# A transformer and expert layer in which attention scores are formed from two exact parts per operand

## The chip, the core and the metric

The kernel runs on one core of a Trainium2 chip. A core has a matrix engine (TensorE, PE in the profile, with its weight loads shown apart as PEld), VectorE (DVE), ScalarE (ACT), GpSimd (POOL) and SyncE (SP), which here only issues DMAs. Each works through its own queue in order; they meet through semaphores. TensorE writes to PSUM, 8 banks of 128 partitions by 512 float32 values. The metric is the device time of one execution in microseconds (us), as the median of several runs.

## The reference, cut to what matters

32 sequences of 256 tokens, 128 features, go through a transformer block (causal self attention, cross attention to one encoder sequence, an MLP) and then through a layer of 8 experts. The change touches the scores and softmax of the two attentions, 16 heads of 8 features:

```python
def _attn_core(q, k, v, extra_bias=None, causal_bool=False, tril_diag2_additive=False):
    w = jnp.einsum('bhqd,bhkd->bhqk', q, k) / jnp.sqrt(jnp.asarray(HD, q.dtype))
    ql, kl = (q.shape[-2], k.shape[-2])
    neg = jnp.finfo(w.dtype).min
    if causal_bool:
        mask = jnp.tril(jnp.ones((ql, kl), bool))
        w = jnp.where(mask[None, None], w, neg)
    if tril_diag2_additive:
        cm = jnp.tril(jnp.ones((ql, kl), w.dtype), k=2)
        w = w + jnp.where(cm == 0, neg, jnp.zeros((), w.dtype))[None, None]
    if extra_bias is not None:
        w = w + extra_bias[:, None, None, :]
    w = jax.nn.softmax(w, axis=-1)
    return jnp.einsum('bhqk,bhkd->bhqd', w, v)
...
a = _attn_core(split_heads(q), split_heads(k), split_heads(v), causal_bool=True)
...
a = _attn_core(split_heads(q), split_heads(k), split_heads(v), extra_bias=scorer_logits, tril_diag2_additive=True)
```

The cross attention's keys and values come from the one encoder sequence, so they are the same for all 32 sequences.

## The kernel before

**Stages.** First the attention of all 32 sequences ("batches" below), self and cross, some 880 us; then the MLP and the gate (`Chunk`), then the experts (`Experts`). The last two are not touched.

**Scores in row groups.** The 16 heads stand in 4 row groups of 4 heads (`NG`, `NJ`). A row group is 32 partitions, and one head takes all 32: 8 features times 4 rows. A float32 query or key is split into three bf16 parts (`projected`, L284 to L287, on GpSimd). Three of the four rows of a feature hold the three parts of the query; the keys repeat one part in those rows. So a head's scores take three bf16 matmuls with 32 rows, one per part of the key (`range(3)` in `maxima` and `weights`), and all nine products of parts are in. The fourth row of each feature is a spare: there masks between blocks of 64 tokens, the logits and the row maxima ride along. Within a block of 64 the causal edge is a separate bf16 matmul with the tables in `strips` (`mask_q`, `mask_k`, `by_q`, `by_k`).

Matmuls of the four row groups run in the array side by side; `issue` (L608) hands them out in turn by their column counts.

**Two passes over the scores.** `maxima` forms scores with queries on the partitions (tile `sc`), and VectorE takes the row maxima (`m`, L483). GpSimd splits them into three bf16 parts (`split`, L489 to L495), TensorE turns them (`turned_maxima`, L501), ScalarE copies them to `mT` (L502) and issues one DMA that puts them in the spare rows of `qs` (L505). `weights` forms scores with keys on the partitions, less the maxima (tile `st`), and ScalarE takes the exponential into `wt` (L545). `weighted` (L564, float32) multiplies by the values and a column of ones; `back`, `turned_back` and `joined` divide, turn and project.

**The way of queries and keys.** `projected` (L279, float32) gives 128 rows; SP stores their parts to DRAM (L290, L292), and after the store has landed loads them back spread over 32 rows per head (`load_queries` L297, `load_keys` L301). Buffers: four each of `qs` per kind of attention, `kr`, and value tiles.

**The order** is written out by hand. A half-step holds one half of an attention's `maxima` (two row groups, all or two of their heads) and one half of another's `weights`, `LAG` = 15 half-steps behind. Two half-steps are issued together (L715 to L729), all four row groups at once, then what follows them (`after`), then the side jobs that `on` and `full` have put at that step. A pair of half-steps fills up to four banks of `sc` and four of `st`, the whole of PSUM; each is free again when VectorE or ScalarE has read it. A self attention has 6 halves, a cross attention 8; in the steady part they alternate, so 14 halves or 7 pairs make a batch. Projections stand at least 8 half-steps ahead of the first use of their queries and keys.

```python
todo = [(nk, t3[:, c, :], self.qs[st, j, qb * P : qb * P + P], self.kr[st, j, part, 0:nk],
         (c, part) == (0, 0)) for c, j in enumerate(js) for part in range(3)]
for a in range(2):
    k0 = qb * P + 64 * a + 2 * self.cross
    w = min(64, nk - k0)
    todo.append((n * w, t3[:, :, k0 : k0 + w], mask_q[st, a, :],
                 by_k[st, 2 : 2 + w].unsqueeze(1).to_broadcast([32, n, w]), False))
```

Of the kernel before, what the change touches and what calls it, by code (L numbers as in the profile page):

```python
# [8 lines left out]
F32 = mybir.dt.float32  # L9
BF16 = mybir.dt.bfloat16  # L10
AF = mybir.ActivationFunctionType
ALU = mybir.AluOpType
# [7 lines left out]
HD = 8  # L20
# [8 lines left out]
V_BUFS = 4  # L29
QK_BUFS = 4  # L30
# [14 lines left out]
def transformer_moe_kernel(ctx: ExitStack, tc: tile.TileContext, ins, out: bass.AP):  # L45
# [54 lines left out]
    strips = const.tile([P, 6 * P + 2 * 66], BF16, name="strips")  # L100
    blocks = strips[:, 0 : 6 * P].rearrange("p (a n) -> p a n", n=P)
    mask_q = blocks[:, 0:2, :]
    mask_k = {False: blocks[:, 2:4, :], True: blocks[:, 4:6, :]}
    by_q, by_k = strips[:, 6 * P : 6 * P + 66], strips[:, 6 * P + 66 : 6 * P + 132]
# [5 lines left out]
    SHIFT = 4  # L110
    q_spare = {cross: const.tile([HD, S], BF16, name=f"q_spare{int(cross)}") for cross in (False, True)}
    k_spare = {}
    div32 = const.tile([P, 4], F32, name="div32")

    def query_spares(cross):
        q = q_spare[cross]
        nc.gpsimd.memset(q, 0.0)
        nc.gpsimd.affine_select(out=q, in_=q, compare_op=ALU.is_ge, fill=NEG, base=0,
                                pattern=[[1, S]], channel_multiplier=-64)
        nc.gpsimd.affine_select(out=q, in_=q, compare_op=ALU.is_ge, fill=0.0, base=SHIFT - 1,  # L120
                                pattern=[[0, S]], channel_multiplier=-1)
        if cross:
            nc.gpsimd.memset(q[0:1], 1.0)

    def key_spares(cross):
        k = k_spare[cross] = scratch([HD, 3, S], BF16, f"k_spare{int(cross)}")
        nc.gpsimd.memset(k, 0.0)
        first = k[:, 0, :]
        nc.gpsimd.memset(first, 1.0)
        for m in (1, -1):  # L130
            nc.gpsimd.affine_select(out=first, in_=first, compare_op=ALU.is_ge, fill=0.0,
                                    base=-2 * cross if m == 1 else 63 + 2 * cross,
                                    pattern=[[m, S]], channel_multiplier=-64 * m)
        nc.gpsimd.affine_select(out=first, in_=first, compare_op=ALU.is_ge, fill=1.0, base=SHIFT - 1,
                                pattern=[[0, S]], channel_multiplier=-1)

    def diagonals():
        def where(t, base, c, m, fill):

            nc.gpsimd.affine_select(out=t[0:32], in_=t[0:32], compare_op=ALU.is_ge, fill=fill, base=base - 2 * m,  # L140
                                    pattern=[[m, 66]], channel_multiplier=c)

        nc.gpsimd.memset(by_q[0:32], HIGH)
        where(by_q, 0, 2, -1, LOW)
        where(by_q, 1, 2, -1, 0.0)
        nc.gpsimd.memset(by_k[0:32], -HIGH)
        where(by_k, -2, -2, 1, -LOW)
        where(by_k, -1, -2, 1, 0.0)

        far = 200 * 31  # L150
        where(by_q, far - 2, -200, -1, LOW)
        where(by_q, far + 62, -200, -1, 0.0)
        where(by_k, far - 2, -200, -1, -LOW)
        where(by_k, far + 62, -200, -1, -HIGH)

    def diagonal_blocks():
        for a in range(2):
            nc.vector.tensor_copy(mask_q[0:32, a, 64 * a : 64 * a + 64], by_q[0:32, 2:66])
            nc.vector.tensor_copy(mask_k[False][0:32, a, 64 * a : 64 * a + 64], by_k[0:32, 2:66])
        nc.vector.tensor_copy(mask_k[True][0:32, 0, 0:66], by_k[0:32])  # L160
        nc.vector.tensor_copy(mask_k[True][0:32, 1, 66:P], by_k[0:32, 2:64])
        for g in range(1, NG):
            nc.sync.dma_start(out=strips[32 * g : 32 * g + 32], in_=strips[0:32])

    def logit_parts():

        left = scratch([1, S], F32, "left")
        parts = k_spare["logits"] = scratch([1, 3, S], BF16, "parts")
        nc.vector.tensor_scalar(left, rows[0:1, R_SC : R_SC + S], -3e38, None, ALU.max)
        for i in range(3):  # L170
            nc.vector.tensor_copy(parts[:, i, :], left)
            if i < 2:
                nc.vector.tensor_tensor(left, left, parts[:, i, :], ALU.subtract)

# [55 lines left out]
    with ExitStack() as actx:  # L230
# [24 lines left out]
        def query_rows(name):  # L255
            return dram.tile([NJ, 32, 4, S], BF16, name=name)

        def key_rows(name):
            return dram.tile([NJ, 32, 4, 3, S], BF16, name=name)

        q_rows = {cross: [query_rows(f"q{int(cross)}{i}") for i in range(QK_BUFS)] for cross in (False, True)}
        k_rows = [key_rows(f"k{i}") for i in range(QK_BUFS)]
        kx_rows = key_rows("kx")

        def fill_spare(d, src):
            n = len(src.shape) - 1
            if n == 1:
                to = d.rearrange("c (g d) i t -> d (c g) i t", d=HD)[:, :, 3, :]
# [27 lines left out]
        def load_queries(t, d):  # L296
            nc.sync.dma_start(out=t, in_=d.rearrange("c m i t -> (m i) c t"))  # L297
# [806 lines left out]
```

## Time and profile before

| | |
|---|---|
| median of 3 runs | 1452.39 us (1451.78 to 1452.43) |
| span of the profiled execution | 1451.7 us |
| granted TensorE clock, mean | 0.987 |
| TensorE busy, share of the span | 1346.3 us, 93% |
| VectorE | 1059.6 us, 73% |
| ScalarE | 870.9 us, 60% |
| GpSimd | 655.3 us, 45% |
| L483, maxima from `sc`, 896 instructions | 493.2 us busy, 607 ns each |
| L545, exponentials from `st`, 896 instructions | 419.8 us busy, 541 ns each |
| DMA | 100.22 MB, mean 69 GB/s |

The profile is of one execution. A row of instructions names its line, engine, operation, the tile written, an arrow and the tiles read, then shapes and counts; `x` counts instructions. Matmul lengths include the way through the array, so rows of one group overlap and sums of lengths exceed the time; where a rate is wanted, the distance between starts tells it. The chain of waits is followed back from the last instruction of a stretch, at each step to what released it.

### The profile page before, as it was taken

How to read it: one execution, taken by the hardware profiler on the slowest of the kernel's cores; microseconds unless marked ns; L12 is line 12 of the kernel's file. 1: busy time of each engine (PE TensorE's matmuls, PEld its weight loads, DVE VectorE, ACT ScalarE, POOL GpSimd, SP SyncE). 2: the span in 40 equal slices, each digit the busy share in tenths (PEclk: the TensorE clock that was granted, in tenths of full speed). 3: DMA queues.
4: the chain of work that ended last, by engine and by line, in shares of the span. 5: the costliest groups of instructions: out<-in, count | busy, mean ns of one | idle time of the engine just before them, and what ended most of it. 6: DMA issues, size and time to landing. Idle time of an engine off the chain costs nothing.

```text
span 1451.7 us, 55993 instructions
## 1 busy us (share of the span) xinstructions
PE 1346.3 (93%) x24028; PEld 963.8 (66%) x24028; DVE 1059.6 (73%) x2959; ACT 870.9 (60%) x2035; POOL 655.3 (45%) x1508
## 2 busy tenths in 40 slices
PE   4798989999999999999999998999899999999996
PEld 3566766776776777677677765777566666666664
DVE  6758878887878888788787761677568666666665
ACT  1366767776777777777676767877345343434343
POOL 7656455555454555545554423886311212121212
PEclk9899999999999999999999999999899999999998
DMA  6643323333242232333322115100000000000000
GB/s 179 183 125 110 112 78 116 101 105 103 86 127 90 84 123 87 109 104 101 100 79 85 35 32 142 36 2 1 1 8 8 15 8 15 8 12 11 9 15 15
DMA packets 115178, 100.22 MB, mean 69 GB/s; under 512 B 5788, under 2 KB 114672, under 8 KB 114928
## 3 DMA queue, kind: packets, MB, share of 16 engines
q1 hardware_dynamic: 104288, 91.17, 20.5%
q10 hardware_dynamic: 10640, 5.47, 1.3%
q8 instruction: 188, 3.08, 0.9%
q14 instruction: 62, 0.51, 0.1%
HBM read 54.47 MB, written 37.77 MB: 64 GB/s over the span
## 4 chain that ended last, share of the span: by engine, by line
PE 63%; DVE 24%; ACT 7%; POOL 4%; issue 2%; ACTq 1%; DMA 0%; POOLq 0%; DVEq 0%; SPq 0%
DVE m L483 14%; PE po L878 9%; PE pa L867 9%; PE pb L868 9%; PE av L564 9%; PE sc L619 8%; PE st L619 5%; ACT wt L545 4%; PE po L991 4%; PE pf L984 3%; PE pq L279 2%; DVE a L587 2%; DVE st L212 1%; DVE xn L225 1%; DVE rec L586 1%
## 5 line engine op out<-in xcount | busy, mean ns | idle before, releaser
L483 DVE TENSOR_REDUCE m<-sc 128x2 f32<-128x512 f32 (+2 forms) x896 | 493.2, 607 | 151.9 <-PE sc L619 92.0
L545 ACT ACTIVATE wt<-st 128x512 f32<-128x512 f32 (+1 forms) x896 | 419.8, 541 | 104.7 <-PE st L619 96.9
L619 PEld LDWEIGHTS <-qs 32*128 32x128 bf16 x6144 | 228.1, 94 | 108.9 <-issue 87.9
L619 PE MATMUL sc<-krx,qs 32*128 32x256 bf16 (+1 forms) x3072 | 185.7, 244 | 26.8 <-ACT xT L250 8.4
L878 PEld LDWEIGHTS po<-w,h 128*128 128x128 f32 x1152 | 155.3, 192 | 69.1 <-issue 50.1
L870 ACT ACTIVATE sa<-pa,cols 128x512 f32<-128x512 f32 x144 | 99.8, 693 | 149.2 <-PE pa L867 121.4
L872 DVE SCALAR_TENSOR_TENSOR h<-pb,cols,sa 128x512 f32<-128x512 f32 x144 | 107.9, 750 | 109.2 <-ACT sa L870 72.8
L619 PE MATMUL st<-qs,krx 32*128 32x256 bf16 (+1 forms) x3072 | 165.0, 243 | 5.9 <-DVE a L587 3.1
L619 PE MATMUL sc<-kr,qs 32*128 32x128 bf16 (+1 forms) x3072 | 164.1, 247 | 2.9 <-DMA kr<-k 1.6
L619 PE MATMUL st<-qs,kr 32*128 32x128 bf16 (+1 forms) x3072 | 160.0, 242 | 6.4 <-DVE m L483 4.3
L878 PE MATMUL po<-w,h 128*128 128x128 f32 x1152 | 162.5, 278 | 0.0
L867 PE MATMUL pa<-h_all,w 128*128 128x512 f32 x288 | 150.6, 605 | 0.0
L868 PE MATMUL pb<-h_all,w 128*128 128x512 f32 x288 | 148.5, 598 | 0.0
L892 POOL TENSOR_TENSOR z<-z 128x512 f32<-128x512 f32 x32 | 41.2, 1287 | 231.3 <-ACT z L888 231.3
L221 POOL TENSOR_TENSOR r<-r,nhalf 128x2 f32<-128x2 f32 (+1 forms) x160 | 133.7, 836 | 13.1
L619 PE MATMUL sc<-strips 32*128 32x128 bf16 (+2 forms) x1792 | 134.8, 223 | 0.1
L619 PEld LDWEIGHTS <-strips 32*128 32x128 bf16 x3584 | 127.8, 94 | 3.4 <-issue 0.5
L619 PE MATMUL st<-strips 32*128 32x128 bf16 (+2 forms) x1792 | 129.8, 222 | 0.0
L220 POOL TENSOR_SCALAR r<-mv 128x2 f32<-128x2 f32 (+1 forms) x160 | 31.1, 195 | 213.0 <-DVE mv L213 191.2
L619 PEld LDWEIGHTS <-kr 32*128 32x128 bf16 x3072 | 112.8, 93 | 14.2 <-issue 13.3
L619 PEld LDWEIGHTS <-krx 32*128 32x128 bf16 x3072 | 106.2, 93 | 13.1 <-issue 12.1
L868 PEld LDWEIGHTS pb<-h_all,w 128*128 128x128 f32 x288 | 55.2, 192 | 69.5 <-issue 58.5
(166 smaller groups left out, 2498.6 us busy)
## 6 DMA issues: line engine op xcount, KB each, us to landing
kr<-k SPq DMA_DIRECT2D x32, 768.0 KB
k<-qkp SPq DMA_DIRECT2D x32, 576.0 KB
qs<-q SPq DMA_DIRECT2D x64, 256.0 KB
q<-qkp SPq DMA_DIRECT2D x64, 192.0 KB
x<-in_x_dram SPq DMA_DIRECT2D x32, 128.0 KB
qs<-mT ACTq DMA_DIRECT2D x64, 64.0 KB
x_all<-in_x_dram SPq DMA_DIRECT2D x8, 512.0 KB
out_dram<-y SPq DMA_DIRECT2D x16, 256.0 KB
```

The source lines that it names most:

```text
L221: nc.gpsimd.tensor_tensor(r, r, nhalf[:, 0:n], ALU.pow)
L483: nc.vector.tensor_reduce(m[:, g, js[0] : js[0] + n], t3, AX.X, ALU.max, negate=True)
L545: nc.scalar.activation(w[:, 0 : n * nq], t, AF.Exp)
L564: nc.tensor.matmul(av[32 * g : 32 * g + 32, at : at + n], lhsT=self.vp[:, kb, g, WINDOW[j] : WINDOW[j] + 32], rhs=self.wts[kb, g, j], star ...
L619: nc.tensor.matmul(dst, lhsT=lhsT, rhs=rhs, start=start, stop=False, skip_group_check=True)
L867: nc.tensor.matmul(pa, lhsT=w1[:, e, 0:D], rhs=rhs, start=True, stop=True)
L868: nc.tensor.matmul(pb, lhsT=w1[:, e, D : 2 * D], rhs=rhs, start=True, stop=True)
L870: nc.scalar.activation(sa, pa, AF.Silu, bias=col(C_B1 + 2 * e))
L872: nc.vector.scalar_tensor_tensor(h, pb, col(C_B1 + 2 * e + 1), sa, ALU.add, ALU.mult)
L878: nc.tensor.matmul(po[:, i, :], lhsT=h[:, i * P : (i + 1) * P], rhs=w2[:, e, :], start=True, stop=e < NE)
L984: nc.tensor.matmul(pf, lhsT=wfc[:, f * P : (f + 1) * P], rhs=self.xT, start=True, stop=True)
L991: nc.tensor.matmul(po[:, i, :], lhsT=self.g[:, f, i * P : (i + 1) * P], rhs=wmlp[:, f, :], start=f == 0, stop=f == FF // P - 1)
```

## The change

Queries and keys become float32 tiles that hold two parts: the value rounded by a cast to float32r on GpSimd, and the float32 remainder. The four rows of a feature in a head's 32 rows hold the four pairs of parts: the query rows repeat (first, second) twice, the key rows hold (first, first, second, second). One float32r matmul per head then has all four products, where three bf16 matmuls stood. There is no spare row any more. Maxima, logits and masks are taken in by a second kind of matmul on bf16 tables of 28 rows per row group: three rows of maxima, three of logits and 22 of a staircase that forms the causal edge for a block of 44 tokens; three such blocks cover 128. They add into the same PSUM banks. `qm` holds the queries' side of the table with the maxima in its first three rows; four small DMAs per attention, issued by ScalarE, put them there. `wc` and `vc` are the tables with logits for the cross attention. Query buffers are shared by both kinds of attention (6), keys have 4, values 3, and the buffer is chosen by which is free first. `values` moves from two steps after the projections to two steps after the first half. The stores of the spare rows (`fill_spare`, `spares`, `encoder_rows`) and `max_frames` are gone.

```diff
-V_BUFS = 4
-QK_BUFS = 4
+V_BUFS = 3
+Q_BUFS = 6
+K_BUFS = 4
+M_BUFS = 2
...
+    RM, RL, R0, RS = 0, 3, 6, 22
+    NR, CW = R0 + RS, 2 * RS
+    NBLK = -(-P // CW)
...
+    def key_edges(cross, kb):
+        off = 2 * cross
+        at = kb * P
+        edges = [at - off if kb else 0] + [at + CW * b - 1 - off for b in range(1, NBLK)] + ([P - off] if kb == 0 else [])
+        return list(zip(edges, edges[1:] + [S], range(NBLK + 1)))
+
+    def query_edges(cross, qb):
+        off, nk = 2 * cross, S if qb else P + 2 * cross
+        at = qb * P + off
+        edges = [0 if cross else at] + [at + CW * b for b in range(1, NBLK)]
+        return list(zip(edges, edges[1:] + [nk], range(NBLK)))
...
-            p = wk.tile([P, n, 3, S], BF16, tag="qkp", name="qkp", bufs=2)
-            nc.gpsimd.tensor_copy(p[:, :, 0, :], x)
-            nc.gpsimd.tensor_tensor(x, x, p[:, :, 0, :], ALU.subtract)
-            nc.gpsimd.tensor_copy(p[:, :, 1, :], x)
-            nc.gpsimd.tensor_tensor(p[:, :, 2, :], x, p[:, :, 1, :], ALU.subtract)
+            p = wk.tile([P, n, S], F32R, tag="qkp", name="qkp", bufs=2)
+            nc.gpsimd.tensor_copy(p, x)
+            nc.gpsimd.tensor_tensor(x, x, p.bitcast(F32), ALU.subtract)
             for i, (_, _, _, _, d) in enumerate(todo):
...
+                to = d.rearrange("c m a t -> a (c m) t")
+                nc.sync.dma_start(out=to[0], in_=p[:, i].bitcast(F32))
+                nc.sync.dma_start(out=to[1], in_=x[:, i])
 
         def load_queries(t, d):
-            nc.sync.dma_start(out=t, in_=d.rearrange("c m i t -> (m i) c t"))
+            for b in range(2):
+                nc.sync.dma_start(out=t.rearrange("(x b) c t -> b x c t", b=2)[b], in_=d.rearrange("c m a t -> (m a) c t"))
 
         def load_keys(t, d):
-            nc.sync.dma_start(out=t.rearrange("p c j t -> p c (j t)"), in_=d.rearrange("c m i j t -> (m i) c (j t)"))
+            for a in range(2):
+                for b in range(2):
+                    nc.sync.dma_start(out=t.rearrange("(m x) c t -> x m c t", x=4)[2 * a + b],
+                                      in_=d.rearrange("c m b t -> b m c t")[b])
...
+        def max_rows(cross):
+            off = 2 * cross
+            for t in qms[cross]:
+                for kb in range(2):
+                    for lo, hi, b in key_edges(cross, kb):
+                        if b < NBLK:
+                            x = U0 + lo - kb * P + off - CW * b
+                            nc.vector.tensor_copy(t[:, :, lo:hi], u_wide[:, x : x + hi - lo].unsqueeze(1).to_broadcast([P, NJ, hi - lo]))
...
-                    todo = [(nk, t3[:, c, :], self.qs[st, j, qb * P : qb * P + P], self.kr[st, j, part, 0:nk],
-                             (c, part) == (0, 0)) for c, j in enumerate(js) for part in range(3)]
-                    for a in range(2):
...
+                    todo = [(nk, t3[:, c, :], self.qs[st, j, qb * P : qb * P + P].bitcast(F32R),
+                             self.kr[st, j, 0:nk].bitcast(F32R), c == 0) for c, j in enumerate(js)]
+                    st = slice(32 * g, 32 * g + NR)
+                    for lo, hi, b in query_edges(self.cross, qb):
+                        w = hi - lo
+                        at = qb * (P + 2)
+                        v = vc[st, at + lo : at + hi] if self.cross else v_wide[st, V0 : V0 + w]
+                        todo.append((n * w, t3[:, :, lo:hi], u_of(b)[st], v.unsqueeze(1).to_broadcast([NR, n, w]), False))
...
                 if qb:
-                    spare = self.qs.rearrange("(x i) j q -> i x j q", i=4)[3]
-                    nc.scalar.dma_start(out=spare, in_=self.mT)
+                    i = self.b % M_BUFS
+                    take(("qm", self.cross, i), self)
+                    self.qm = qms[self.cross][i]
+                    for g in range(NG):
+                        nc.scalar.dma_start(out=self.qm[32 * g : 32 * g + 3], in_=self.mT[12 * g : 12 * g + 12])
...
-                        for part in range(3):
-                            todo.append((nq, t3[:, c, :], self.kr[st, j, part, kb * P : kb * P + P],
-                                         self.qs[st, j, q0:S], (c, part) == (0, 0)))
...
+                        todo.append((nq, t3[:, c, :], self.kr[st, j, kb * P : kb * P + P].bitcast(F32R),
+                                     self.qs[st, j, q0:S].bitcast(F32R), c == 0))
+                    st = slice(32 * g, 32 * g + NR)
+                    for lo, hi, b in key_edges(self.cross, kb):
+                        w = (wc[:, kb, b, :] if self.cross else v_of(b))[st]
+                        todo.append((n * (hi - lo), t3[:, :, lo - q0 : hi - q0], w, self.qm[st, js[0] : js[0] + n, lo:hi], False))
...
-                full(e + 2, 0.55, x.values)
+                full(s + 2, 0.55, x.values)
```

Beside what the cut shows: `stairs` builds the staircase tables on GpSimd at the first step and spreads them by three DMAs; `logit_rows` fills `wc` and `vc` with some 15 copies on VectorE and 15 DMAs from SP at step 5, and `max_rows` fills the `qm` tiles with 12 copies on VectorE for each kind of attention, at steps -1 and 3.

## The prediction

> **What bounds the kernel now.** I read the stretch by engine first, then one period of the attention step by step, then the chain of waits, and last the rows that price what the change puts in. The windows view of the steady attention (120 to 840 us; columns: length, then busy time of TensorE, its weight loads, VectorE, ScalarE and GpSimd, granted clock, DMA share, GB/s):
>
> ```profile
> 120.00:840.00 720.00, 676.19 (x18400) 505.87 (x18400) 586.68 (x1473) 511.22 (x1249) 373.38 (x995) 1.00 0.31 96
> ```
>
> TensorE is busy 94%, VectorE 81%, ScalarE 71%, at full clock. A busy TensorE includes latencies, so I counted its work: in one batch (one self and one cross attention) each of the four row groups streams 22,576 columns of scores and masks. The timeline starts four 256-column bf16 matmuls, one per row group, every 0.107 us, so 0.418 ns per column, 9.4 us a batch. Seven pair steps make a batch; the same view, cut at the first score matmul of each step:
>
> ```profile
> 491.24:493.56 2.32, 2.32 (x88) 1.94 (x85) 1.45 (x4) 1.71 (x5) 0.00 (x0) 1.00 0.23 81
> 493.56:497.55 3.99, 3.89 (x111) 2.72 (x111) 3.92 (x12) 2.90 (x6) 2.05 (x8) 1.00 0.36 101
> 497.55:501.51 3.96, 3.63 (x102) 2.96 (x100) 3.50 (x6) 2.60 (x6) 1.53 (x6) 1.00 0.08 22
> 501.51:505.79 4.28, 3.83 (x99) 2.52 (x99) 3.44 (x11) 3.28 (x7) 2.99 (x4) 1.00 0.01 4
> 505.79:508.54 2.75, 2.75 (x80) 2.46 (x77) 2.02 (x6) 2.12 (x5) 2.22 (x7) 1.00 0.48 175
> 508.54:513.50 4.96, 4.04 (x99) 2.59 (x100) 2.63 (x8) 3.07 (x10) 3.43 (x11) 1.00 0.86 253
> 513.50:517.22 3.72, 3.72 (x104) 2.77 (x101) 2.75 (x6) 2.44 (x5) 1.48 (x3) 1.00 0.31 108
> sum 25.98, PE 24.19 PEld 17.96 DVE 19.73 ACT 18.10 POOL 13.70; mean PE 3.46 PEld 2.57 DVE 2.82 ACT 2.59 POOL 1.96
> ```
>
> The reader is to see that no engine bounds all steps. The second is VectorE's (3.92 of 3.99 us); the first, fifth and seventh are TensorE's. The chain of waits over the same 720 us says how much of the scores lies on the path, and the waits say who waits for them:
>
> ```profile
> by line: DVE m L483 25.0%; PE sc L619 15.2%; PE av L564 14.6%; PE st L619 9.4%; ACT wt L545 6.9%; DVE a L587 3.0%; PE pq L279 2.8%; DVE xn L225 2.0%; issue 2.0%; DVE rec L586 1.8%; DVE st L212 1.8%; ACT xT L250 1.7%; DVE h_all L225 1.7%; PE
> ```
> ```profile
> PEld L619 <- issue: 96.3, 332, 0.8
> ACT wt L545 <- PE st L619: 86.4, 194, 1.3
> DVE m L483 <- PE sc L619: 70.8, 75, 1.7
> DVE m L483 <- PE st L619: 53.4, 50, 6.1
> ```
>
> L619 has 24.6% of 720 us, 177 us; over 720 / 25.98 = 27.7 batches that is 6.4 us of its 9.4 us, a share of 0.68. VectorE and ScalarE both wait for it.
>
> **The change part by part.** *Score matmuls.* 96 bf16 matmuls per batch and row group become 32 on float32r, half of them 256 columns wide, half 128 or 130. No float32r matmul runs in the kernel before; the nearest rows are float32 (timeline of TensorE: start, length, line, count):
>
> ```profile
> 500.22 0.38 PE L580 MATMUL pa<-ident,avs 128*128 128x128 f32 x2
> 500.44 0.22 PE L501 MATMUL pt_m<-ident_b,mparts 128*128 128x128 bf16 x1
> 500.49 1.08 PE L279 MATMUL pq<-xT,wqkv 128*128 128x256 f32 x4
> 501.51 0.28 PE L619 MATMUL sc<-kr,qs 32*128 32x256 bf16 x2
> 501.51 0.28 PE L619 MATMUL st<-qs,kr 32*128 32x256 bf16 x2
> ```
>
> Two float32 transposes of 128 columns (0.27 us each by itself) end 0.38 us after the first starts, so they start 0.11 us apart. The four of L279 (0.43 us the first) start (1.08 - 0.43) / 3 = 0.217 us apart at 256 columns: twice the bf16 pace, and two such instructions make one float32 product (the page counts 288 at L867 for 144 activations at L870). So a float32 product is four passes at bf16 pace, a transpose, whose identity needs no second half, two. Bounds for the 32: at bf16 pace 16 x 0.053 + 16 x 0.107 = 2.6 us; as one float32 instruction each 16 x 0.11 + 16 x 0.217 = 5.2 us; as whole float32 products 10.4 us. I take 32 x 0.11 = 3.5 us: one rounded operand on either side leaves one pass (0.053 or 0.107), but 128 four-byte weights were not seen loading oftener than every 0.11 us. That loads and passes of the four row groups overlap is seen for bf16 here, and for float32 only across column groups (L564).
>
> The Trainium skill, "FP8 and Floating Point Precision" (TensorE Precision Notes), says that true FP32 takes four passes and that there is a mode which reads four bytes and truncates. The four passes agree with the rows above; no row shows the reduced mode. Against the change stands "TensorE: Matmul & The Clock Gate" (Weight-path perf modes, LDWEIGHTS): the fast weight load is not given to FP32, and a load then takes columns / 1.2 ns, an estimated 107 ns for 128. The rows have loads of 93 ns in bf16, 140 to 190 ns in float32. By that rule the 32 would be 3.4 us, by the bf16 row alone 2.6 us.
>
> *Masks, maxima, logits.* 28 bf16 mask matmuls (4,096 of the 22,576 columns) become 46 staircase ones of 5,648 columns: 5,648 x 0.418 = 2.4 us at least, 3.0 us if each takes at least the 0.053 us of a 128-column one; 2.6 us taken, since few are below 80 columns. Sum 3.5 + 2.6 = 6.1 us against 9.4: 3.3 us less per batch (bounds: 9.4 - 5.0 = 4.4 less, 13.4 - 9.4 = 4.0 more). On the path 3.3 x 0.68 = 2.2 us. The self steps cannot use all of it: the second has 0.07 us of VectorE slack against some 0.6 us saved, so 0.5 x 0.68 = 0.3 us is lost there and VectorE's maxima are next in line. 1.9 us.
>
> *ScalarE's queue.* The maxima go out in four DMAs per attention instead of one. Rows by tile:
>
> ```profile
> L505 ACTq DMA_DIRECT2D qs<-mT x64: 537/537/626, 45.9 to 872.1; - x64
> L768 SPq DMA_DIRECT2D bias<-in_rb_dram x12: 272/290/308, 907.4 to 914.5; - x12
> ```
>
> Each issue holds ScalarE, and behind it wait exponentials and with them the score banks. Four of 12 short rows each are nearest to L768 (8 rows): 4 x 0.29 - 0.54 = 0.62 us more per attention (at 0.25 us, the cheapest issue seen, 0.46; at 0.54, 1.6). Twice a batch that is 1.25 us on an engine that is off the path for most of its time (some 10% of the chain); a block of 1.2 us at a stretch hurts more than its share, so a quarter: 0.3 us (0.1 to 1.6).
>
> *SP's queue.* A self attention issues four stores and six loads instead of two and two, 0.33 to 0.43 us each; bytes are about the same (768 KB stored and 1,024 loaded become 512 and 1,024). GpSimd's split loses one cast and one subtraction (L286, L287: 0.61 + 1.16 us), which pays the 2.2 us of extra issues. Before, the key load is issued 5.3 to 10.6 us ahead of the first matmul that uses it, and the first one ever landed 5.0 us after its issue, so alternate batches have almost nothing spare. I cost this at nothing (-0.3 to +1.6 us); the cover is that slack, and a faster step eats it.
>
> *Steps and start.* The hand-written order gives the same sequence of self and cross attentions, 464 half-steps instead of 466. In the first 120 us L286 and L287 go from the chain (5.3%, 6.4 us), while VectorE gets 24 staircase copies and some 15 for the logits (about 0.2 us each, as L197), half on the path: -3 us. SP's 15 issues for the logits at step 5 take the place of 14 for the spare rows: nothing.
>
> *Sum.* 1.9 - 0.3 = 1.6 us per batch, times 32 = 51 us, and 3 at the start: 1451.7 - 54 = 1398 us of span; the median lies 0.7 us above the span, 1398 with that after rounding. VectorE would then be at 19.7 / 24.4 = 81%, up from 76% of this period.
>
> **The rivals.** *B, float32r at the pace of one float32 instruction* (5.2 us): for it, every float32 instruction here moves at half pace; against it, the count of passes. 9.4 - 7.8 = 1.6 saved, 1.1 on the path, 0.8 net, 26 us: 1424. *E, the transfers or ScalarE's queue take the gain*: key loads come 1.6 us late in each batch, as alternate ones are near to; 1449, no change. *C, the other side: float32r is paid as a float32 product* in L607's matmuls (two instructions, four passes; perhaps only for the narrow ones, which would be B's time). TensorE then has 13.4 - 9.4 = 4.0 us more per batch and is the bound in every step; 3.2 us of that shows, 102 us: about 1553. It decides from 0.2 us per float32r matmul on: 32 x 0.2 + 2.6 + 0.44 (0.3 us of path at 0.68) is the old 9.4 us. Against it: nothing is gained by a rounded operand then. *D, float32r matmuls of different row groups do not overlap*: 4 x 3.5 + 2.6 = 16.6 us, 7 us more per batch, beyond 1650. A drain at each change between float32r and bf16 would act alike, but the rows show a bf16 transpose between float32 work with no gap (starts at 500.33, 500.44, 500.49).
>
> **How the numbers follow.** A 0.57, B 0.13, E 0.06, C 0.17, D 0.05, and 0.02 for late transfers that cost more than is won. A's own range is 1355 (all 4.4 us at 0.68 less 0.1 us on ScalarE, 2.9 x 32 = 93 us, and the start) to 1424, where it meets B. The whole range runs from 1350 (a start worth 5 us more) to 1500: B and E are in it, C and D, about 0.2, mostly out. What a measurement of this kernel can tell from no change is about 0.2%, 3 us. Faster 0.70, within 0.06, slower 0.24.
>
> **What would show it.** Score matmuls on float32r starting about 0.11 us apart within a row group and four groups together; scores below a fifth of the steady chain, VectorE's maxima above a quarter; attention ending near 830 us instead of 880; L496 issues near 0.29 us. It would be wrong if the float32r rows show two instructions per call or starts 0.2 us apart, if ScalarE's issues are 0.54 us each with exponentials late behind them, or if score matmuls wait for key or query loads in every batch.

## The result and the profile after

| | before | after |
|---|---|---|
| median, us (4 runs each) | 1452.41 (1451.78 to 1455.3) | 1614.05 (1609.21 to 1618.61) |
| ratio, 95% interval | 1 | 1.1112 (1.1087 to 1.1137) |
| span of the profiled execution, us | 1451.7 | 1616.9 |
| end of the attention, us from the start | 888.8 | 1052.5 |
| TensorE at half clock before that, us | 21 | 276 |
| maxima DMAs on ScalarE per attention | 1 of 0.54 us | 4 of 0.73 us |

The change makes the kernel 11% slower. The forecast was 1398 us, within 1350 to 1500, so both its direction and its range were wrong. Of the 165.2 us between the two spans, 163.7 lie in the attention stage.

The windows view of the steady attention after the change (columns as in the forecast's first fence):

```profile
120.00:840.00 720.00, 601.92 (x10839) 432.74 (x10832) 480.45 (x1219) 409.37 (x1025) 254.21 (x736) 0.85 0.26 82
```

Every engine is less busy than before. TensorE has gone from 94% to 84%, VectorE from 81% to 67%, ScalarE from 71% to 57%. A longer time with no busier engine means waiting; the chain of waits over the same 720 us names its place:

```profile
by line: PE av L552 14.8%; ACTq L496 13.3%; PE sc L607 11.8%; ACT wt L532 10.4%; DVE m L470 10.3%; PE st L607 7.3%; PE pq L281 6.8%; issue 4.1%; PE pa L568 3.6%; DMA qs<-q 2.6%; PE po L590 2.5%; PE pv L331 1.8%; ACT xT L264 1.7%; ACT qk L28
```

The second entry is new. ACTq is ScalarE's queue while it issues DMAs, and L496 is the line of the four maxima DMAs: 13.3%, 95.8 us of 720. The scores have gone from 24.6% to 19.1%, VectorE's maxima from 25.0% to 10.3%. The row of that line, by tile (columns: shortest, median and longest issue in ns):

```profile
L496 ACTq DMA_DIRECT2D qm<-mT x256: 728/729/1367, 39.1 to 1035.9; - x128
```

The forecast took 0.29 us for each. One block of four, in the timeline (start, length, what; in brackets the idle time before it and what ended it; other rows left out):

```profile
499.75 3.06 ACTq L496 DMA_DIRECT2D qm<-mT  x4
...
502.86 0.56 ACT L264 ACTIVATE xT<-pt_x,cols 128x256 f32<-128x256 f32 x1 [3.14 <-DMA qm<-mT]
...
503.48 0.38 PE L607 MATMUL sc<-krx,qs 32*128 32x256 f32 x2 [2.90 <-ACT xT L264]
...
504.26 0.69 DVE L470 TENSOR_REDUCE m<-sc 128x2 f32<-128x512 f32 x1 [2.94 <-PE sc L607]
```

ScalarE does nothing but issue for 3.06 us. It then makes a copy, 0.06 us after which TensorE's next scores start, idle for 2.90 us by then; VectorE, which needs those scores, had waited 2.94 us. The three engines stop for the same 3 us. The waits of ScalarE over the 720 us show that this is the rule (columns: total us, times, longest us):

```profile
ACT xT L264 <- DMA qm<-mT: 73.2, 22, 4.3
...
ACT avs L557 <- DMA qm<-mT: 37.7, 12, 3.4
...
ACT vpad L334 <- DMA qm<-mT: 34.5, 11, 3.4
```

These are 45 waits of 3.2 us, and the stretch holds 720 / 31.6 = 22.8 batches of two attentions: one such wait per attention. One period of seven pair steps, cut as the one of before:

```profile
510.68:512.80 2.12, 2.12 (x54) 1.82 (x50) 1.43 (x4) 1.70 (x5) 0.00 (x0) 1.00 0.18 35
512.80:518.04 5.24, 4.00 (x83) 2.68 (x82) 5.17 (x14) 2.74 (x6) 2.86 (x10) 1.00 0.35 114
518.04:524.36 6.32, 5.18 (x66) 3.75 (x62) 4.29 (x11) 2.92 (x8) 0.74 (x4) 0.77 0.03 6
524.36:527.84 3.48, 3.44 (x79) 2.43 (x78) 1.96 (x4) 3.17 (x7) 2.25 (x4) 0.92 0.22 75
527.84:530.12 2.28, 2.28 (x56) 1.82 (x52) 1.67 (x5) 1.80 (x4) 1.29 (x4) 1.00 0.45 154
530.12:537.99 7.87, 5.31 (x75) 3.10 (x74) 2.89 (x9) 2.79 (x9) 3.89 (x11) 0.82 0.48 145
...
```

The two blocks of this period start at 516.7 and 530.9 us. The steps that hold them (second to third, and sixth) take 11.56 and 7.87 us, where they took 7.95 and 4.96; the other steps shown are 0.2 to 0.8 us shorter than before. So the lighter scores do show, where no block stands. The granted clock is the second new thing: 0.77, 0.92 and 0.82 in three of these steps, 1.00 in all seven before.

### The profile page after: what moved, and what is told of

It reads as the page before. It is cut to its first block, busy times and chain, and to the rows that moved or that the text cites. A ratio compares the mean times of both kernels' runs of the same rounds, so it can differ in the third digit from the quotient of the medians.

```text
span 1616.9 us, 44868 instructions
## 1 busy us (share of the span) xinstructions
PE 1413.8 (87%) x18140; PEld 990.8 (61%) x18140; DVE 1056.7 (65%) x2988; ACT 856.7 (53%) x2035; POOL 558.5 (35%) x1333
## 4 chain that ended last, share of the span: by engine, by line
PE 64%; DVE 11%; ACT 9%; ACTq 8%; issue 3%; DMA 2%; POOL 2%; SPq 0%; POOLq 0%; DVEq 0%
PE av L552 10%; PE po L863 8%; ACTq L496 8%; PE pa L852 8%; PE pb L853 8%; PE sc L607 7%; DVE m L470 7%; ACT wt L532 6%; PE st L607 5%; PE pq L281 4%; PE po L976 4%; PE pf L969 3%; PE pa L568 2%; PE po L590 2%; DMA qs<-q 1%
## 5 line engine op out<-in xcount | busy, mean ns | idle before, releaser
L607 PE MATMUL sc<-krx,qs 32*128 32x256 f32 (+1 forms) x1024 | 151.8, 345 | 50.8 <-ACT xT L264 37.8
L607 PE MATMUL sc<-kr,qs 32*128 32x128 f32 (+1 forms) x1024 | 134.7, 343 | 36.4 <-ACT avs L557 15.4
L607 PEld LDWEIGHTS sc<-krx,qs 32*128 32x128 f32 x1024 | 99.2, 208 | 92.7 <-ACT xT L264 39.8
L607 PE MATMUL st<-qs,krx 32*128 32x256 f32 (+1 forms) x1024 | 136.7, 337 | 6.7 <-DVE a L575 3.8
L607 PEld LDWEIGHTS sc<-kr,qs 32*128 32x128 f32 x1024 | 89.8, 208 | 75.2 <-issue 28.0
L607 PE MATMUL st<-qs,kr 32*128 32x256 f32 (+1 forms) x1024 | 127.2, 346 | 4.1 <-DVE m L470 3.0
L607 PEld LDWEIGHTS <-stairs 28*128 28x128 bf16 x4096 | 126.6, 105 | 6.4
L557 ACT COPY avs<-av 128x256 f32<-128x256 f32 x128 | 47.5, 371 | 140.3 <-PE av L552 77.1
L552 PE MATMUL av<-wt,vpadx 128*32 128x256 f32 (+1 forms) x2048 | 108.8, 359 | 14.0 <-DVE m L470 12.4
L552 PE MATMUL av<-wt,vpad 128*32 128x256 f32 (+1 forms) x2048 | 116.4, 377 | 0.1
```

What stands on the lines that cost most here:

```text
L552: nc.tensor.matmul(av[32 * g : 32 * g + 32, at : at + n], lhsT=self.vp[:, kb, g, WINDOW[j] : WINDOW[j] + 32], rhs=self.wts[kb, g, j], star ...
L607: nc.tensor.matmul(dst, lhsT=lhsT, rhs=rhs, start=start, stop=False, skip_group_check=True)
```

## The experiments

**Where the four DMAs are issued.** Two kernels move them, with one word changed: to SP (`nc.sync`), and to GpSimd (`nc.gpsimd`). A third leaves the kernel before as it is and adds only three such DMAs on ScalarE, to a tile that nobody reads.

```diff
-                        nc.scalar.dma_start(out=self.qm[32 * g : 32 * g + 3], in_=self.mT[12 * g : 12 * g + 12])
+                        nc.sync.dma_start(out=self.qm[32 * g : 32 * g + 3], in_=self.mT[12 * g : 12 * g + 12])
```

> The changed kernel with the four small maxima DMAs of each attention issued by SP instead of ScalarE; nothing else differs. Theory Q (ScalarE's queue: four issues of 0.73 us, 3.1 us in a row, hold exponentials and score banks, and TensorE's idle spells then halve its clock): the 3.1 us blocks go, the mean granted clock of TensorE comes back from 0.91 to above 0.97, and the time falls from 1614 to between 1425 and 1465 us. Rival F (the float32r matmuls and their weight loads are the loss): the time stays above 1550 us and the clock below 0.93. Rival S (SP's queue, held by the wait for the maxima, delivers queries and keys late): 1480 to 1540 us, with score matmuls waiting for DMAs.

Measured: 1443.48 us (1442.51 to 1444.87), 0.9936 of before (0.9920 to 0.9952). The move gives back 171 us, as theory Q had it. The clock did not follow: it is 0.94 to 0.96 over the four runs, up from 0.91, where above 0.97 was expected.

> The changed kernel with the four maxima DMAs issued by GpSimd (busy 35% after the change) instead of ScalarE. Theory Q: 1425 to 1470 us, clock above 0.97; slower than with SP only if an issue costs GpSimd more than 1 us, as its splits then come late. Rival F: above 1550 us.

Measured: 1510.59 us (1501.45 to 1517.10), 1.0393 (1.0349 to 1.0436), above the 1425 to 1470 us expected; an issue of over 1 us was to be the condition for that, and it takes 0.545. It holds GpSimd 140 us in all, and the kernel takes 67 us more than with SP. Its chain has the issue itself and GpSimd's split of the maxima (`mparts`, `mr`):

```profile
by line: PE av L552 20.2%; DVE m L470 16.5%; PE sc L607 11.9%; PE st L607 5.8%; issue 5.0%; POOL qm L496 4.4%; PE pq L281 4.2%; POOL h_all L409 3.4%; POOL r L235 3.2%; POOL mparts L480 3.1%; ACT wt L532 2.8%; POOL mr L482 2.5%; PE pt_m L489
```

The kernel before with three more DMAs (buffers of `x` 5 to 4 and of `mT` 5 to 3, to make room for the tile):

```diff
                     nc.scalar.dma_start(out=spare, in_=self.mT)
+                    for g in range(1, NG):
+                        nc.scalar.dma_start(out=dummy[32 * g : 32 * g + 3], in_=self.mT[12 * g : 12 * g + 12])
```

> The kernel before with three more small DMAs per attention on ScalarE's queue, into a scratch tile that nobody reads (12 rows of 512 bytes each, the form that the change issues); two tile pools are one to two buffers smaller to make room. Theory Q: three issues of 0.73 us on top of the 0.54 us make 2.7 us blocks, so the kernel before loses most of what the change lost: 1530 to 1600 us, clock below 0.95. Rival F: the issues are hidden, 1452 to 1475 us, clock still above 0.98.

Measured: 1595.79 us (three runs at 1595.6 to 1596.5, one at 1572.44), 1.0930 (1.0845 to 1.1015). 64 attentions times 3 issues of 0.723 us are 139 us of ScalarE, and the kernel is 143 us slower by the median, 119 by its fastest run. Its chain shows the added line (L508) and the old one (L506):

```profile
by line: PE av L567 14.4%; PE sc L622 13.8%; ACTq L508 13.7%; ACT wt L548 9.9%; DVE m L484 9.5%; PE st L622 9.3%; ACTq L506 3.8%; issue 3.4%; PE pq L279 2.6%; PE pa L583 2.0%; PE pt_a L596 1.9%; DVE xn L225 1.7%; ACT xT L250 1.6%; DVE a L59
```

The scores there are those of before, so the issues, with no float32r in the kernel, make most of the loss. The smaller buffers of this kernel were not tried alone. With the move to SP, which undoes the loss from the other side, the cause is settled.

**Time on the queue, or a block of it?** The same issues as after, on ScalarE, but two right away and two a pair of half-steps later; and two on ScalarE with two on SP.

```diff
-                    for g in range(NG):
-                        nc.scalar.dma_start(out=self.qm[32 * g : 32 * g + 3], in_=self.mT[12 * g : 12 * g + 12])
+                    self.sent(0)
+
+            def sent(self, h):
+                for g in (2 * h, 2 * h + 1):
+                    nc.scalar.dma_start(out=self.qm[32 * g : 32 * g + 3], in_=self.mT[12 * g : 12 * g + 12])
...
+                if qb:
+                    on(e + 2, x.sent, 1)
```

> The changed kernel with all four DMAs on ScalarE, but two at the old place and two a pair of half-steps later: the same issues and the same 3.1 us per attention, in two blocks of 1.5 us. Proportional: within 20 us of 1614 us. Threshold: 1470 to 1560 us, clock above 0.94. Rival: the second pair lands too late for the first score matmul that reads it, and the time stays or grows with matmuls waiting for DMAs.

Measured: 1508.46 us (1501.96 to 1514.34), 1.0379 (1.0342 to 1.0416), inside the range put for a threshold; its clock, 0.93 to 0.94, is a little under the 0.94 expected. 256 issues of 0.729 us as after, and yet 106 us of the 171 are gone. Its chain over 120 to 840 us, where the issues (L499) have 7.0% for 13.3%:

```profile
by line: DVE m L470 19.0%; PE av L555 18.0%; PE sc L610 13.4%; ACT wt L535 9.5%; ACTq L499 7.0%; PE st L610 6.7%; PE pq L281 3.5%; PE pa L571 2.3%; issue 2.2%; DVE a L578 2.2%; ACT xT L264 2.0%; DVE xn L239 1.7%; PE po L593 1.5%; PE pt_a L5
```

```diff
-                        nc.scalar.dma_start(out=self.qm[32 * g : 32 * g + 3], in_=self.mT[12 * g : 12 * g + 12])
+                        eng = nc.scalar if g < 2 else nc.sync
+                        eng.dma_start(out=self.qm[32 * g : 32 * g + 3], in_=self.mT[12 * g : 12 * g + 12])
```

> The changed kernel with two of the four maxima DMAs of each attention on ScalarE and two on SP: ScalarE is held 1.5 us at a stretch instead of 3.1. Theory Q with a cost in proportion to ScalarE's held time: half way between 1443 us (none on ScalarE) and 1614 us (four), 1515 to 1545 us. Theory Q with a threshold (short blocks hide behind full banks, only those of 3 us empty the queues and halve TensorE's clock): 1440 to 1490 us.

Measured: 1511.01 us (1505.36 to 1513.96), 1.0393 (1.0365 to 1.0420), between the two ranges expected: under that of a cost in proportion, over that of a threshold. One block of 1.5 us per attention costs what two of them with starts mostly 2.8 to 3.5 us apart cost, 68 and 65 us over SP, and one of 3.1 us costs 171. That a second short block comes free, where the same time in one piece does not, is what these runs show. Slack of ScalarE after each block would explain it; that is argued, and which wait takes it up was not followed.

**What the change is worth without the block.** For a fair comparison the kernel before gets the same move, its one maxima DMA on SP:

```diff
-                    nc.scalar.dma_start(out=spare, in_=self.mT)
+                    nc.sync.dma_start(out=spare, in_=self.mT)
```

> The kernel before with its one maxima DMA per attention issued by SP instead of ScalarE (64 issues of 0.54 us, 34 us of ScalarE's time). Theory: one issue of 0.54 us is mostly hidden on ScalarE, 1440 to 1453 us. Rival: ScalarE's queue is a bound in the kernel before as well: 1415 to 1435 us, and the change then has no gain of its own left beside it.

Measured: 1439.84 us (1438.04 to 1440.67), 0.9908 (0.9888 to 0.9927), at the lower end of what was expected. It is as fast as the change on SP (0.9936). So the float32r scores buy nothing in the end, where the forecast had 61 us (1.9 us times 32). Where their gain goes, the windows view of two batches (14 pair steps) shows: the kernel before on SP, then the change on SP, first two batches without a spell of half clock and then two with one:

```profile
587.23:637.58 50.35, 48.51 (x1329) 36.42 (x1326) 42.33 (x105) 36.60 (x90) 27.33 (x72) 1.00 0.34 106
229.49:278.40 48.91, 45.52 (x960) 33.37 (x956) 41.77 (x113) 36.02 (x90) 23.73 (x68) 1.00 0.34 107
587.07:638.23 51.16, 48.10 (x960) 35.46 (x957) 41.13 (x105) 36.22 (x90) 22.12 (x64) 0.93 0.33 102
```

At full clock the change gains 1.44 us in two batches, 23 us in 32. But from 308 to 776 us a spell of 6.8 us at half clock stands in every two batches, and they take 2.25 us more: two neighbouring steps grow from 7.85 to 10.2 us together, the others stay within about 0.1. The kernel before on SP has no spell from 206 us to the end of its attention. So the scores do gain at full clock, and the clock takes the gain back.

Over the whole stretch the change on SP has full engines and a clock below one; its chain, beside it, has the scores at 23.1%:

```profile
120.00:840.00 720.00, 672.91 (x13512) 494.52 (x13512) 579.12 (x1492) 510.87 (x1271) 306.86 (x898) 0.94 0.31 98
```
```profile
by line: DVE m L470 21.9%; PE av L552 21.0%; PE sc L607 14.5%; PE st L607 8.6%; PE pq L281 4.8%; ACT wt L532 3.1%; PE pa L568 2.8%; PE pv L331 2.6%; issue 2.5%; PE pt_a L581 2.2%; DVE a L575 1.9%; PE pt_m L489 1.8%; PE po L590 1.7%; ACT qk 
```

To price the float32r matmul itself, one kernel on SP reads only the upper half of each float32 part as bf16, in the same loops. It leaves the lower 16 bits of every part out of the scores.

```diff
-                    todo = [(nk, t3[:, c, :], self.qs[st, j, qb * P : qb * P + P].bitcast(F32R),
-                             self.kr[st, j, 0:nk].bitcast(F32R), c == 0) for c, j in enumerate(js)]
+                    todo = [(nk, t3[:, c, :], half(self.qs)[st, j, qb * P : qb * P + P],
+                             half(self.kr)[st, j, 0:nk], c == 0) for c, j in enumerate(js)]
```

> The kernel with SP's maxima, whose score matmuls read the upper halves of the same tiles as bf16 (one pass, every second element): the lower bits of all parts are left out, masks, maxima and logits stay. Measures what float32r costs against one bf16 pass. From the changed kernel's trace a float32r matmul in a row group takes its columns at full rate and then 0.11 us of weight load that is not hidden: 6.1 us per batch, bf16 2.6 us. If that is right and 0.68 of it is on the path: 60 to 80 us faster than with SP's maxima alone. Rival: VectorE's maxima and ScalarE hold the pace anyway, less than 25 us faster.

Measured: 1383.88 us (1380.68 to 1393.84), 0.9548 (0.9508 to 0.9588): 60 us faster than float32r with the same count of matmuls, columns and DMAs, at the lower end of what was expected. Two of its batches at full clock:

```profile
595.50:642.23 46.73, 42.69 (x961) 28.64 (x958) 41.17 (x106) 35.74 (x90) 22.08 (x64) 1.00 0.35 109
```

That is 2.18 us less than float32r's 48.91, or 35 us in 32 batches: what the format costs against one bf16 pass. The rest goes with the clock, at half for 19 of the 720 us here and for 89 in the change on SP. TensorE's timeline in one cross step shows the format's part; first the change on SP, then this kernel (`sc` in two row groups at a time):

```profile
505.67 0.38 PE L607 MATMUL sc<-krx,qs 32*128 32x256 f32 x2
505.67 0.39 PE L607 MATMUL st<-qs,krx 32*128 32x256 f32 x2
505.89 0.28 PE L607 MATMUL sc<-krx,qs 32*128 32x256 f32 x2
...
506.01 0.32 PE L607 MATMUL sc<-vc,stairs 28*128 28x348 bf16 x2
```
```profile
502.05 0.29 PE L610 MATMUL sc<-krx,qs 32*128 32x256 bf16 x2
...
502.18 0.27 PE L610 MATMUL sc<-krx,qs 32*128 32x256 bf16 x2
...
502.29 0.31 PE L610 MATMUL sc<-vc,stairs 28*128 28x348 bf16 x2
```

In both the row groups start together. Two float32r matmuls of 256 columns start 0.22 us apart in a row group, two bf16 ones 0.13 here, and the staircase follows the last after 0.12 and 0.11 us. So the first float32r matmul takes 0.11 us more and the second next to nothing; their lengths, 0.38 and 0.28 us, say the same. In the same run four of 128 columns stand in a row:

```profile
509.61 0.30 PE L607 MATMUL sc<-kr,qs 32*128 32x128 f32 x2
...
509.75 0.28 PE L607 MATMUL sc<-kr,qs 32*128 32x128 f32 x2
...
509.87 0.39 PE L607 MATMUL sc<-kr,qs 32*128 32x128 f32 x4
```

The last row holds the third and the fourth, 0.11 us apart. Call such an unbroken row of float32r matmuls in one row group a series. Over all series at full clock in the change on SP, the second starts 0.22 us (256 columns) or 0.16 us (130) after the first, the third and fourth (128 columns) about 0.11 us after the one before, and a staircase follows the last after 0.12 us at every width. The columns alone need 0.107 and 0.054 us at 0.42 ns each. One reading fits all of these: the first float32r matmul of a series shows its weight load of 0.11 us in full; the later loads run beside the columns of the matmul ahead, and the longer of the two sets the pace. In the kernel with bf16 halves a matmul starts only 3 to 19 ns later than the columns ahead of it need.

**Can the 0.11 us be hidden?** One theory was that the weights of a float32r matmul can't load while another float32r matmul of its row group runs, and would load behind a bf16 one. So the two kinds take turns:

```diff
-                    work[g] = todo
+                    work[g] = mixed(todo, n)
...
+        def mixed(todo, n):
+            out = []
+            for i in range(max(n, len(todo) - n)):
+                out += todo[i : i + 1] if i < n else []
+                out += todo[n + i : n + i + 1]
+            return out
```

> The kernel with SP's maxima, and within each tile the float32r matmuls and the staircase matmuls take turns (float32r, staircase, float32r, staircase, ...) instead of all float32r first. The same instructions, another order. In the changed kernel's trace a second float32r matmul in a row group starts 0.22 us (256 columns) or 0.16 us (130) after the first, its columns at full rate plus 0.11 us, while one behind a staircase matmul starts 0.03 us after it. Theory L (the weight load of a float32r matmul isn't hidden behind a float32r matmul of its row group, but is behind a bf16 one): 18 such pairs per batch, 2.0 us, 0.68 on the path: 30 to 55 us faster than with SP's maxima alone, that is 1390 to 1415 us. Rival M (float32r itself costs 0.11 us more, wherever it stands, or VectorE holds the pace): within 12 us of 1443 us.

Measured: 1438.03 us (1434.57 to 1440.02), 0.9897 (0.9876 to 0.9918), 5 us better than without turns, and not the gain that the theory needed. From a float32r matmul to a staircase the excess over the columns is now 95 to 117 ns, where it was 16 ns behind the second of two wide ones. With a bf16 matmul ahead, nearly all of the 32 show their load, not only the first of each series: a bf16 matmul doesn't hide it, another float32r one does. At full clock the turns cost a little, 0.31 us in two batches:

```profile
578.32:627.54 49.22, 47.05 (x960) 34.18 (x956) 41.16 (x105) 36.12 (x90) 22.20 (x64) 1.00 0.34 106
```

Fewer spells of half clock go with the 5 us won: 38 us of the 720 in this trace, 89 without turns. Two more kernels send the maxima in three DMAs of 16 rows, all row groups at once, instead of four of 12, with turns and without:

```diff
-                    for g in range(NG):
-                        nc.scalar.dma_start(out=self.qm[32 * g : 32 * g + 3], in_=self.mT[12 * g : 12 * g + 12])
+                    for i in range(3):
+                        nc.sync.dma_start(out=self.qm.rearrange("(g x) j q -> x g j q", x=32)[i], in_=self.mT[16 * i : 16 * i + 16])
```

> As the run with turns, and the maxima go out in three DMAs of 16 rows (one per part, all four row groups) instead of four of 12. SP saves one issue of 0.70 us per attention. Theory: SP's queue is no bound, within 6 us of the run with turns. Rival S (SP's queue delivers late): 8 to 25 us faster than it.

> Three DMAs of 16 rows on SP, with the float32r matmuls first as in the change. Theory: within 6 us of the 1443 us with four DMAs on SP. Rival S: 8 to 25 us faster.

Measured: 1443.17 us (1441.73 to 1444.91), 0.9935 (0.9918 to 0.9952) with turns, and 1437.42 us (1432.29 to 1443.26), 0.9896 (0.9859 to 0.9934) without. Turns help by 5 us with four DMAs and cost 6 with three, but the runs of the last kernel alone lie up to 11 us apart. At full clock two batches take 48.8 to 48.9 us with three DMAs as with four, so SP's queue is no bound here. No order that was tried got below 1437 us.

**Two bf16 parts.** If it is the format that costs, two parts in bf16 should have the gain of one pass, and stores and loads of half the bytes. This leaves the third part of every query and key, its last 8 bits, out of the scores.

```diff
-            p = wk.tile([P, n, S], F32R, tag="qkp", name="qkp", bufs=2)
-            nc.gpsimd.tensor_copy(p, x)
-            nc.gpsimd.tensor_tensor(x, x, p.bitcast(F32), ALU.subtract)
+            p = wk.tile([P, n, 2, S], BF16, tag="qkp", name="qkp", bufs=2)
+            nc.gpsimd.tensor_copy(p[:, :, 0, :], x)
+            nc.gpsimd.tensor_tensor(p[:, :, 1, :], x, p[:, :, 0, :], ALU.subtract)
...
-                to = d.rearrange("c m a t -> a (c m) t")
-                nc.sync.dma_start(out=to[0], in_=p[:, i].bitcast(F32))
-                nc.sync.dma_start(out=to[1], in_=x[:, i])
+                nc.sync.dma_start(out=d.rearrange("c m a t -> (c m) a t"), in_=p[:, i])
```

> The changed kernel with SP's maxima and two bf16 parts per query and key in place of the float32r ones: one bf16 pass per head, half the bytes, one store per operand; the third part of the kernel before, the last 8 bits, is left out of the scores. If the bf16 pass reading every second element showed float32r's whole price, it comes to 1370 to 1395 us and beats both kernels, at some loss of precision in the scores; VectorE's maxima are then the largest part of the chain. If strided reading or the lateness of transfers cost something there, down to 1350 us.

> The kernel with two bf16 parts and SP's maxima (1382 us; the last 8 bits of queries and keys are left out of the scores), with three maxima DMAs of 16 rows in place of four of 12. If SP's queue is no bound here either: within 6 us of 1382 us. If the maxima come late at the faster pace: 1360 to 1375 us.

Measured: 1381.59 us (1378.76 to 1382.04), 0.9501 (0.9484 to 0.9518), and with three maxima DMAs of 16 rows 1374.07 us (1371.13 to 1375.35), 0.9460 (0.9443 to 0.9477). Both beat both kernels. Half the bytes add little: 1382 beside the 1384 of the kernel with bf16 halves. The second is in the range put for maxima that come late, but that is not shown: two batches at full clock take 46.6 us in both, and where the 8 us between them arise was not followed. The chain of the first, where the scores have 12.3% and VectorE's maxima are the largest entry, as the forecast had for its own case:

```profile
by line: DVE m L468 31.2%; PE av L550 18.9%; PE sc L605 8.3%; PE st L605 4.0%; ACT wt L530 3.4%; DVE a L573 3.2%; PE pt_a L579 2.3%; DVE xn L239 2.1%; DVE rec L572 2.0%; issue 1.9%; DVE st L226 1.8%; DVE h_all L239 1.7%; PE pa L566 1.7%; PE
```

## Why the prediction was wrong

**"ScalarE's queue" is the step that failed**, in its price and in its share.

- The price, "Four of 12 short rows each are nearest to L768 (8 rows): 4 x 0.29 - 0.54 = 0.62 us more per attention", came from a DMA that SP issues to another place. The DMA nearest in its data was L505, the one that was replaced: from `mT`, on ScalarE, 0.54 us. The new ones, of 12 rows, take 0.729 us each, more than the single one of 128 rows, and a block of four 3.06 us: 2.5 us more per attention, 5.0 per batch, four times the 1.25 taken and beyond the upper end of 1.6 per attention. Reading the cost as one that falls with the rows was the error. On SP the same DMA takes 0.70 us, so it isn't ScalarE alone.
- The share, "a quarter", was the graver part. By its average ScalarE was off the path, but a block holds whatever stands behind it, and here that was the copy without which neither the next scores nor the maxima start. The chain has 95.8 / 22.8 = 4.2 us per batch on the path, of 6.1 us of issues. With the right price and a quarter the sum would still have been a gain: 1.9 - 0.25 x 5.0 = 0.65 us a batch. With the whole 5.0 us it is a loss of 3.1 us, 99 us in 32 batches, 1551. The text named the danger ("a block of 1.2 us at a stretch hurts more than its share") and still priced it at a quarter; the runs with blocks of 1.5 us (65 to 68 us) and of 3.1 us (171 us) show what it costs.
- The rest is the clock, which the forecast left at its 1.00. During the attention TensorE is granted half clock for 276 us after, 150 with the DMAs on SP. At most half of the difference of 126 us can be lost time, 63 us. The chain's share of the issues, 13.4% over the 932 us from 120 us to the end of the attention, is 125 us. 171 us lie between 125 and 125 + 63. The kernel with two blocks of 1.5 us bears this out: its half clock, 154 us, is nearly that on SP, and its issues' 7.0% of 819 us are 57 of the 65 us that it loses to SP. The split for the change itself is an estimate from these views.

**"Score matmuls": the mechanism held, a term was missing.** One instruction per float32r matmul, row groups together, one pass over the columns: all as forecast. So is 0.11 us as the pace within a series, the longer of load and columns. Left out was the first load of each series, which nothing covers: a batch has 14 series in a row group, so 14 x 0.11 = 1.5 us on top of 3.5. By the measured starts, 8 series of two wide ones take 0.346 us each, 4 of two narrow ones 0.28 and 2 of four 0.50: 4.9 us for the 32, near rival B's 5.2. The prediction's own row had a sign of it. It divided the four matmuls of L279 into even distances of 0.217 us; taken one by one in that trace they start 0.27, 0.22 and 0.22 us apart. "TensorE: Matmul & The Clock Gate" of the Trainium skill (LDWEIGHTS) puts a load at columns / 1.2 ns, an estimated 107 ns for 128; the 0.11 us measured here agree.

B's time (26 us won) was reached where the clock stayed full, 23 us, and the half clock took it back: 89 us of the steady attention against 7 in the kernel before on SP. One step grew at full clock, the second of the period, from 3.99 to 5.24 us; VectorE has 5.17 us of work in it after (14 instructions), 3.92 before (12), and fills it both times. Most others took less, by up to 0.8 us. Why the clock halves is open. With bf16 halves in the same loops it is at half for 19 us, none of them between 131 and 800 us.

**"Masks, maxima, logits"**, 2.6 us: 5,648 columns and an excess of about 7 ns between staircases make 2.7 us. Right.

**The gain forecast for the score step came true with bf16 halves, in part by luck.** Two batches take 46.73 us there and 50.35 in the kernel before on SP, 1.8 us per batch, where the forecast had 1.9. But the 32 score matmuls take some 2.9 us there (2.57 of columns and about 0.01 each), not 3.5; with that the forecast's share of 0.68, less its 0.3, would have given 2.3. So the share on the path was too large, and that made up for it.

**"SP's queue"**: transfers late by little. `qs<-q` has 2.6% of the chain after, some 19 us of 720, within the -0.3 to +1.6 us per batch given to it (19 / 22.8 = 0.8). On SP the chain's first entries hold no transfer, so E is no part of the answer.

**The rivals.** B had nearly the right cost of float32r and was not the cause of the loss. C (two instructions, four passes) and D (row groups in turn) are excluded by the starts above. The rival on the slow side should have been the one that lost its place in the sum: ScalarE's queue as a stall. It had been given 1.6 us per batch at most and a part of E's 0.06. **Of the signs named ahead**, "ScalarE's issues are 0.54 us each with exponentials late behind them" came true, and worse; "starts 0.2 us apart" came true for the two wide matmuls of a series, 0.22. One sign of being right, "scores below a fifth of the steady chain", also came true, with 19.1%, but because the issues had made the whole longer.

## What to carry to other kernels

An issue of a DMA cost ScalarE and SP more here for 12 rows than for 128; splitting one DMA into four multiplied that cost. So price it by the row of the very engine and tile, and put such DMAs on a queue with nothing behind it. A block on an engine's queue can cost far more than the engine's average share says, once it is longer than the slack of the engines that wait behind it; look for what stands next in its queue. A format that needs fewer passes isn't priced by its passes alone: count the weight loads that nothing covers, here the first of each series. And compare stretches at the same granted clock, or a gain in one place and a loss of clock in another look like nothing at all.

## What the runs showed that was not expected

- **The cost of an issue**: 0.729 us on ScalarE, 0.70 on SP and 0.545 on GpSimd for 12 rows of 512 bytes, 0.57 on SP for 16 rows, and 0.54 on ScalarE and SP for the old single DMA of 128 such rows. A query load onto every second partition takes SP 0.625 us and a key load onto every fourth 0.60, where one onto all 128 took 0.36.
- **Four-byte weights**: the first float32r matmul of a series shows its load of 128 weight columns, 0.11 us, in each row group by itself, while the row groups overlap. Behind another float32r matmul the load is hidden up to that one's columns; behind a bf16 one it isn't.
- **Half clock without an idle TensorE.** In the change on SP, spells of 6.8 us at half clock return every 51.2 us, although TensorE's rows leave it idle for only 0.6 of the 6.8 us before one. The records stand on a grid of 3.413 us, and 51.2 us are 15 of them, two batches. "TensorE: Matmul & The Clock Gate" (Part 1, the HAM clock gate) has that window, and gives a half clock to one that was idle; here one that was busy by its rows got it. What it counts as busy stays open. How a slow clock looks: in the block at 530.9 us after the change, the 32 matmuls of `av` behind it took 2.79 us, where they take 1.51 at full clock.
